# Gated layers of a local-attention block: the 42 features beyond five full tiles, packed two token halves side by side on TensorE

## The chip, the cores and the metric

The kernel runs on one core of one Trainium2 chip, as one launch. The metric is device microseconds of that launch. Five engines are named as in the profile: PE (TensorE matmuls; PEld are its weight loads), DVE (VectorE), ACT (ScalarE), POOL (GpSimd) and SP (SyncE, which issues most DMAs). All data are 32-bit floats.

## The reference, cut to what matters

The network has four stages on 8 sequences of 512 tokens with 256 features: differential attention, a local-attention transformer of two layers, a diffusion stage and a mixture of experts. Only the second half of each layer of the second stage is touched:

```python
HID = int(DIM * 4 * 2 / 3)          # 682
def _layer(x, wqkv, qs, ksc, wo, lg, lb, w1, b1, w2, b2):
    ...
    x = x + o @ wo
    h = shift_token(x)
    mu = h.mean(-1, keepdims=True)
    var = h.var(-1, keepdims=True)
    h = (h - mu) / jnp.sqrt(var + 1e-05) * lg + lb
    h = h @ w1 + b1                 # 256 -> 2 * 682
    a, g = jnp.split(h, 2, axis=-1)
    h = a * jax.nn.gelu(g, approximate=False)
    x = x + h @ w2 + b2             # 682 -> 256
    return x
for l in range(DEPTH):              # DEPTH = 2
    x = _layer(x, ...)
```

682 is five times 128 and 42 left over.

## The kernel before, in words

A tile has 128 partitions (`P`). A sequence is held as four token tiles (`NT = 4`, `S = 512` tokens). The second stage is `local`; it works through 16 combinations of layer and sequence, `combos`, layer 0 for all eight sequences and then layer 1. Three strands are laid into each other by hand: `rotated(c + 1)` (projections, normalised and rotated queries and keys of the next combination), `scores`/`turned`/`attend` (attention of the present one, eight steps `u` as listed in `slots`) and `gated(c - 1)` (output projection and the gated layers of the one before). `rotated` and `gated` are generators; each `yield` ends a part, and `slots` says at which step a part is taken. Within the hand-made order a scheduler sets the final order of each engine's queue.

All matmul results of this stage come from one PSUM pool, `big`, of four buffers, each of two banks (`two` gives a tile of 128 x 2 x 512). The buffers go round, so a new tile waits until the engine that reads the tile four before is done.

`gated` does this for one combination. It multiplies the attention output by `wo` (L680, tile `lpp<-lwo,loT`), adds it to x (L681), moves half the features down by one token with two DMAs into `hs` (L685, L686), normalises (L691), and transposes into `ghT` with ACT applying scale and bias (L694, L546). Then come the gated layers:

- First layer, L697 to L707. For each of six chunks of hidden features, `HCH`, four matmul calls fill a tile `lpa`: two halves (i = 1 the gate, i = 0 the value) by two slices of 128 input features. The stationary operand is a slice of `w1`, the moving one 512 tokens of `ghT`. ACT takes gelu of the gate half (L702, tile `gl`), DVE adds the bias to the value half and multiplies (L703) into `hid` (named `u` in the profile). The sixth chunk has 42 features, so its stationary operand has 42 columns.
- Second layer, L708 to L714. For each pair of token tiles, a tile `lpp` gets for each of the two token tiles six matmul calls of 256 output features, with `hid` as the stationary and `w2` as the moving operand; the sixth chunk has 43 rows, 42 features and a row of ones that carries the bias b2. DVE adds the tile to x (L714).

All these calls go through the helper `mm`, so the profile books them on L200; they are told apart by tile and shape. One matmul call on 32-bit floats appears in the profile as two matmul records with a weight load each: `lpa` has 16 x 6 x 4 = 384 calls and 768 records. Below, "record" means one of these.

The weights of a layer are loaded by `load_local` (L490), by DMAs on SP's queue, into a pool with one buffer for each name; so layer 1 is loaded when `gated(8)` begins, as the last readers of layer 0 let go. The tile `hid` is one buffer for the whole stage; its ones are set once by a memset (L726).

Elsewhere in this stage small operands already share the array: `lsc` (L619) multiplies two heads whose 64 features lie in partitions 0 to 63 and 64 to 127, and `lpo` (L667) writes two heads of 64 features to partitions 0 to 63 and 64 to 127 of one bank.

Of the kernel before, what the change touches and what calls it, by code (L numbers as in the profile page):

```python
# [9 lines left out]
F32 = mybir.dt.float32  # L10
BF16 = mybir.dt.bfloat16
AF = mybir.ActivationFunctionType
ALU = mybir.AluOpType
# [3 lines left out]
P = 128  # L17
NB = 8
NT = 4
S = P * NT  # L20
D = 256
DC = D // P
# [4 lines left out]
FH = 8  # L27
FL = 2
HID = int(D * 4 * 2 / 3)
HCH = [(m, min(P, HID - m)) for m in range(0, HID, P)]  # L30
TH = 16
CH = 8
NE = 8
# [5 lines left out]
HOLD = 1000  # L39
# [77 lines left out]
class Net:  # L117
# [372 lines left out]
    def load_local(self, w, l):  # L490
        nc, a = self.nc, self.a
        g = {}
        g["wo"] = w.tile([P, 4, D], F32, name=f"lwo{l}", tag="wo")
        nc.sync.dma_start(g["wo"], a["L0_ffn_wo"][l].rearrange("(c p) f -> p c f", p=P))
        g["w1"] = w.tile([P, DC, 2 * HID], F32, name=f"lw1{l}", tag="w1")
        nc.sync.dma_start(g["w1"], a["L0_ffn_w1"][l].rearrange("(c p) f -> p c f", p=P))
        n, full = len(HCH), HID // P
        g["w2"] = w.tile([P, n, D], F32, name=f"lw2{l}", tag="w2")
        nc.sync.dma_start(g["w2"][:, :full, :], a["L0_ffn_w2"][l][:full * P].rearrange("(c p) f -> p c f", p=P))
        nc.sync.dma_start(g["w2"][:HID - full * P, full, :], a["L0_ffn_w2"][l][full * P:])  # L500

        nc.sync.dma_start(g["w2"][HID - full * P:HID - full * P + 1, full, :], a["L0_ffn_b2"][l].unsqueeze(0))
        g["b1"] = w.tile([P, 2, n], F32, name=f"lb1{l}", tag="b1")
        for i in range(2):
            b1 = a["L0_ffn_b1"][l][i * HID:(i + 1) * HID]
            with nc.allow_non_contiguous_dma(reason="a bias"):
                nc.sync.dma_start(g["b1"][:, i, :full], b1[:full * P].rearrange("(c p) -> p c", p=P))
                nc.sync.dma_start(g["b1"][:HID - full * P, i, full:], b1[full * P:].unsqueeze(1))
        with nc.allow_non_contiguous_dma(reason="a scale"):
            g["g"] = self.column(w, a["L0_ffn_ln_g"][l], DC, "lg")  # L510
            g["b"] = self.column(w, a["L0_ffn_ln_b"][l], DC, "lb")
        return g

    def local(self, nb, early, first):
# [3 lines left out]
        with ExitStack() as ctx:  # L518
            pool = lambda n, b, **k: ctx.enter_context(self.tc.tile_pool(name=n, bufs=b, **k))
            w = pool("wlocal", 1)  # L520
            wk, small = pool("l_wk", 2), pool("l_small", 4)
            big, dram = pool("l_big", 4, space=PSUM), pool("l_x", 1, space=bass.MemoryType.DRAM)
            nc, tc = self.nc, self.tc
# [4 lines left out]
            two = lambda name: big.tile([P, 2, S], F32, name=name, tag="big")  # L528
# [7 lines left out]
            def flipped(src, dsts, scale=None, bias=None):  # L536

                pt = two("lpt")
                for c in range(DC):
                    for t in range(NT):  # L540
                        nc.tensor.transpose(pt[:, c, self.tok(t)], src[:, t, self.tok(c)], self.ident)
                for c, dst in enumerate(dsts):
                    if scale is None:
                        self.copy(dst, pt[:, c, :])
                    else:
                        nc.scalar.activation(dst, pt[:, c, :], AF.Identity, bias=bias[:, c:c + 1], scale=scale[:, c:c + 1])  # L546
# [110 lines left out]
            def attend(c, h):  # L657
# [10 lines left out]
                                             rhs=pT[:, i, self.tok(t + k)], start=k == max(t - 1, 0), stop=k == t)  # L668
                nc.scalar.copy(attended[c][:, h, :], po[:, 0, :])

            def gated(c):

                l, b = combos[c]
                if l not in rest:
                    rest[l] = self.load_local(w, l)
                g, y = rest[l], self.xb(b)
                oT = attended.pop(c)
                pp = two("lpp").rearrange("p i (t d) -> p (i t) d", d=D)
                for t in range(NT):
                    self.mm(pp[:, t, :], [(oT[:, i, self.tok(t)], g["wo"][:, i, :]) for i in range(4)])  # L680
                nc.vector.tensor_add(y, y, pp)  # L681

                hs = wk.tile([P, NT, D], F32, name="hs", tag="hs", bufs=1)
                nc.gpsimd.memset(hs[0:1, 0, P:D], 0.0)
                nc.sync.dma_start(hs[1:P, :, P:D], y[0:P - 1, :, P:D])  # L685
                nc.sync.dma_start(hs[0:1, 1:NT, P:D], y[P - 1:P, 0:NT - 1, P:D])  # L686
                nc.gpsimd.tensor_copy(hs[:, :, 0:P], y[:, :, 0:P])
                yield

                with tc.issue_after(last[0]), tc.issue_after(last[1]):  # L690
                    self.norm_rows(small, hs, hs)  # L691
                yield
                hT = wk.tile([P, DC, S + 1], F32, name="ghT", tag="hT")
                flipped(hs, (hT[:, 0, 0:S], hT[:, 1, 0:S]), g["g"], g["b"])  # L694
                yield
                rows = [n + (m == len(HCH) - 1) for m, (_, n) in enumerate(HCH)]
                for m, (m0, n) in enumerate(HCH):  # L697
                    pa = two("lpa")
                    for i in (1, 0):
                        self.mm(pa[:n, i, :], [(g["w1"][:, c, i * HID + m0:i * HID + m0 + n], hT[:, c, 0:S]) for c in range(DC)])  # L700
                    gl = wk.tile([P, S], F32, name="gl", tag="gl")
                    gelu = nc.scalar.activation(gl[:n, :], pa[:n, 1, :], AF.Gelu, bias=g["b1"][:n, 1, m:m + 1])  # L702
                    nc.vector.scalar_tensor_tensor(hid[:n, m, :], pa[:n, 0, :], g["b1"][:n, 0, m:m + 1], gl[:n, :], ALU.add, ALU.mult)  # L703
                    if m % 3 == 2:
                        with tc.issue_after(gelu.ins):
                            nc.scalar.preload_act_table_set("natural_log_exp_and_others")
                        yield  # L707
                for t0 in range(0, NT, 2):  # L708
                    if t0:
                        yield  # L710
                    pp = two("lpp").rearrange("p i (t d) -> p (i t) d", d=D)
                    for t in range(2):
                        self.mm(pp[:, t, :], [(hid[:n, m, self.tok(t0 + t)], g["w2"][:n, m, :]) for m, n in enumerate(rows)])
                    nc.vector.tensor_add(y[:, t0:t0 + 2, :], y[:, t0:t0 + 2, :], pp[:, 0:2, :])  # L714
                if l == FL - 1:
                    xs = wk.tile([P, NT, D], F32, name="lx", tag="hs", bufs=1)
                    nc.sync.dma_start(xs, saved[b])
                    self.norm_rows(small, y, y)
                    nc.gpsimd.tensor_add(y, y, xs)

            first, second = Between(), Between()
            r, g = first, second
            total = len(combos)
            self.logs = True
            hid = w.tile([P, len(HCH), S], F32, name="u", tag="u")
            nc.gpsimd.memset(hid[32:64, len(HCH) - 1, :], 1.0)  # L726
            for b in range(min(2, nb)):
                save(b)
            for b in range(min(2, nb)):
# [5 lines left out]
            for c in range(total + 1):  # L735
                if c + 1 < total:
                    r.add(rotated(c + 1))
                for u, calls in enumerate(slots):
                    if c < total:
                        scores(c, u)  # L740
                    if u == 2 and c:
                        g.add(gated(c - 1))
                    half = (len(calls) + 1) // 2
                    for f in calls[:half]:
                        f()
                    before = (c, u - 1) if u else (c - 1, 7)
# [735 lines left out]
```

## Time and profile before

| | |
|---|---|
| time, median of 3 runs | 3997.38 us (3994.92 to 3998.51) |
| the profiled execution, its own time | 3997.02 us |
| its span, first to last instruction | 3995.3 us |
| PE busy | 3578.1 us (90%) |
| DVE, ACT, POOL busy | 2220.8, 1837.3, 1593.6 us (56%, 46%, 40%) |
| mean granted TensorE clock | 0.944 |
| first and last matmul of `lpa` | 1338.6 and 2735.9 us |
| last addition of `lpp` to x (L714) | 2748.5 us |
| DVE L703 on 128 x 512, mean of one | 750 ns |
| ACT gelu L702 on 128 x 512, mean of one | 687 ns |

The stage of the change fills the stretch from about 1176 to 2752 us of the span. Engines work at the same time, so their busy times do not add up; a stretch is bounded by the engine that has no gaps in it, or by the chain of waits through it. [...] what a record takes from PE's time is the distance from its start to the next start.

### The profile page before, as it was taken

How to read it: one execution, taken by the hardware profiler on the slowest of the kernel's cores; microseconds unless marked ns; L12 is line 12 of the kernel's file. 1: busy time of each engine (PE TensorE's matmuls, PEld its weight loads, DVE VectorE, ACT ScalarE, POOL GpSimd, SP SyncE). 2: the span in 40 equal slices, each digit the busy share in tenths (PEclk: the TensorE clock that was granted, in tenths of full speed). 3: DMA queues.
4: the chain of work that ended last, by engine and by line, in shares of the span. 5: the costliest groups of instructions: out<-in, count | busy, mean ns of one | idle time of the engine just before them, and what ended most of it. 6: DMA issues, size and time to landing. Idle time of an engine off the chain costs nothing. (4 is left out here: it accounts for less than half of the span.)

```text
span 3995.3 us, 53421 instructions
## 1 busy us (share of the span) xinstructions
PE 3578.1 (90%) x20002; PEld 1915.7 (48%) x20002; DVE 2220.8 (56%) x4380; ACT 1837.3 (46%) x3671; POOL 1593.6 (40%) x1427
## 2 busy tenths in 40 slices
PE   8999999999978999999999999986988888769985
PEld 3343434443335555555555555553444444446654
DVE  6777767776645666665555555543344343345445
ACT  3555555555434444444444444433554555323334
POOL 3666666666644333333333333311012211143333
PEclk8999999999978999999999999997998999879997
DMA  9200000000000000000000000000000000421114
GB/s 363 87 1 6 6 6 1 6 6 6 6 32 1 3 4 5 4 3 25 9 30 9 9 9 9 9 9 29 6 17 19 25 17 17 133 67 55 54 44 161
DMA packets 92878, 130.46 MB, mean 33 GB/s; under 512 B 23040, under 2 KB 71238, under 8 KB 92614
## 3 DMA queue, kind: packets, MB, share of 16 engines
q1 hardware_dynamic: 86086, 109.10, 8.1%
q0 software_dynamic: 6528, 17.87, 1.3%
q8 instruction: 162, 2.65, 0.3%
q14 instruction: 102, 0.84, 0.1%
HBM read 57.58 MB, written 65.18 MB: 31 GB/s over the span
## 5 line engine op out<-in xcount | busy, mean ns | idle before, releaser
L359 ACT ACTIVATE e<-sa 128x1024 f32<-128x1024 f32 (+3 forms) x512 | 359.2, 702 | 344.6 <-PE sa L352 342.2
L380 POOL TENSOR_TENSOR e<-e,e 128x1536 f32<-128x1536 f32 (+2 forms) x192 | 451.6, 2352 | 93.9 <-PE po L375 83.9
L352 PE MATMUL sa<-qT,kT 32*128 32x512 f32 (+3 forms) x2048 | 435.5, 502 | 8.5 <-ACT e L359 8.1
L342 PE MATMUL sc<-kT,qT 32*128 32x128 f32 (+3 forms) x2048 | 425.4, 498 | 8.8 <-DVE spread L356 5.3
L356 DVE TENSOR_REDUCE spread<-sc 128x2 f32<-128x256 f32 (+3 forms) x512 | 422.2, 825 | 15.3
L200 PE MATMUL lpa<-ghT,lw 128*128 128x512 f32 (+1 forms) x768 | 344.1, 603 | 18.1 <-ACT ghT L546 18.1
L633 ACT ACTIVATE lp<-lp,lnm 128x256 f32<-128x256 f32 (+1 forms) x512 | 240.0, 470 | 261.1 <-DVE lnm L625 165.8
L637 POOL TENSOR_TENSOR lp<-lp,lrs 128x1024 f32<-128x1024 f32 x64 | 121.1, 1893 | 552.3 <-DVE lrs L634 552.3
L355 DVE TENSOR_TENSOR sc<-sc,const 128x256 f32<-128x256 f32 x512 | 218.6, 427 | 163.8 <-PE sa L352 140.3
L342 PEld LDWEIGHTS sc<-kT,qT 32*128 32x128 f32 x2048 | 161.3, 190 | 284.9 <-issue 127.3
L1011 ACT ACTIVATE te<-tsa 128x1024 f32<-128x1024 f32 x256 | 250.3, 1023 | 70.4 <-PE tsa L1007 63.5
L200 PE MATMUL lqk<-qkv,lhT 128*128 128x512 f32 x512 | 245.5, 618 | 2.3 <-DVE qk L584 1.6
L585 POOL TENSOR_TENSOR qk<-qk,over 128x1024 f32<-128x1024 f32 x64 | 151.3, 2365 | 220.8 <-DVE qk L584 220.8
L200 PEld LDWEIGHTS lpa<-ghT,lw 128*128 128x128 f32 (+1 forms) x768 | 134.3, 180 | 212.7 <-issue 169.8
L362 POOL TENSOR_SCALAR_AFFINE_SELECT e<-e 128x512 f32<-128x512 f32 x256 | 160.2, 639 | 174.3 <-ACT e L359 174.2
L1324 ACT ACTIVATE ehT<-eht,enorm 128x128 f32<-128x128 f32 x288 | 108.2, 457 | 209.3 <-PE eht L1320 208.3
L200 PE MATMUL lpp<-lw,u 128*128 128x256 f32 (+1 forms) x768 | 193.2, 396 | 0.0
L375 PE MATMUL po<-e,v 128*32 128x512 f32 (+3 forms) x2048 | 189.1, 453 | 4.0 <-POOL e L362 3.6
L622 DVE TENSOR_TENSOR lp<-lsc,const 128x768 f32<-128x768 f32 (+1 forms) x128 | 138.7, 1083 | 93.2 <-PE lsc L619 93.1
L619 PE MATMUL lsc<-lkT,lqT 64*128 64x256 f32 (+1 forms) x1024 | 158.5, 389 | 27.6 <-DVE qk L584 27.5
L352 PEld LDWEIGHTS sa<-qT,kT 32*128 32x128 f32 x2048 | 160.9, 191 | 43.4 <-ACT e L359 26.7
L1007 PE MATMUL tsa<-tqT,tkT 32*128 32x512 f32 x1024 | 160.4, 675 | 12.6 <-DVE tqT L968 12.0
(278 smaller groups left out, 6850.1 us busy)
## 6 DMA issues: line engine op xcount, KB each, us to landing
xrows<-zero SPq DMA_DIRECT2D x66, 514.0 KB
ex<-xrows SPq DMA_DIRECT2D x72, 128.5 KB
ew<-in_L_ffn_w_dram SPq DMA_DIRECT2D x16, 512.0 KB
egot<-yrows SPq DMA_DIRECT2D x16, 512.0 KB
x<-in_L_attn_X_dram SPq DMA_DIRECT2D x8, 512.0 KB
saved<-x SPq DMA_DIRECT2D x8, 512.0 KB
lx<-saved SPq DMA_DIRECT2D x8, 512.0 KB
xf<-xf SPq DMA_DIRECT2D x8, 512.0 KB
```

Of the source, the lines that this page charges most:

```text
L200: self.nc.tensor.matmul(out, lhsT=l, rhs=r, start=i == 0, stop=i == len(pairs) - 1)
L342: nc.tensor.matmul(sc[:, i, :w], lhsT=qT[g, self.tok(t)], rhs=kT[g, :w], start=True, stop=True)
L352: nc.tensor.matmul(sa[:, i, :S - k * P], lhsT=kT[g, self.tok(k)], rhs=qT[g, k * P:], start=True, stop=True)
L355: nc.vector.tensor_add(sc[:, :, w - P:w], sc[:, :, w - P:w], own)
L356: nc.vector.tensor_reduce(self.spread[n % 2][:, t, g0:g0 + 2, 0 if n % 2 else 16], sc[:, :, :w], AX.X, ALU.max, negate=True)
L359: nc.scalar.activation(x[:, h0:h0 + 2, :], sa[:, :, :S - k * P], AF.Exp, scale=0.25)
L362: nc.gpsimd.affine_select(x[:, :, :P], x[:, :, :P], [[0, 4], [1, P]], ALU.is_ge, 0.0, base=0, channel_multiplier=-1)
L375: nc.tensor.matmul(pos[n][group(g), k * P:], lhsT=seqs[b][1][:, k, 4 * r + g, :], rhs=x[:, g, :], start=k == 0, stop=k == 2)
L380: nc.gpsimd.tensor_add(y, y, es.pop((n, k)))
L633: nc.scalar.activation(x, x, AF.Exp, bias=nm[:, i, k:k + 1], accum_out=rs[:, i, k:k + 1])
L1007: m = nc.tensor.matmul(sa[i // 2][:, i % 2, :], lhsT=kT[q, self.tok(k)], rhs=qT[q, :], start=True, stop=True)
L1011: nc.scalar.activation(e[:, 2 * i:2 * i + 2, :], sa[i], AF.Exp)
```

## The change

The last chunk of 42 features is taken out of the loop over equal chunks. In the first layer its 512 tokens are split into two sets, the tokens of the even and those of the odd token tiles, 256 each. Both sets are multiplied by the same 42 weight columns, filled up with zeros to 64: one call writes its result to partitions 0 to 63 of `lpa`, the other to partitions 64 to 127, in columns 0 to 255. So eight calls of 64 weight columns and 256 tokens stand for four calls of 42 columns and 512 tokens. ACT's gelu works on 128 x 256 for 42 x 512; DVE writes two results of 42 x 256, to partitions 0 to 41 and 64 to 105 of a new tile `left` (named `uleft`), whose rows 42 and 106 are ones.

In the second layer the two token tiles of a pair now have a bank each. Each gets five calls of 128 rows, first the one tile, then the other, and then the two calls of 43 rows follow each other, the first on partitions 0 to 42, the second on 64 to 106. `together` keeps the second call of such a pair right behind the first.

The leftover weights get tiles of their own: `r1` (`lr1`), zeroed by POOL before its DMAs, and `r2` (`lr2`), which holds the 42 rows of w2 and the bias row twice. The bias tile `b1` is zeroed too and holds its last 42 entries twice. `load_local` issues 18 DMAs instead of 11, and POOL gets two memsets per layer; the ones are set by two memsets of 32 x 256 instead of one of 32 x 512.

In the order of PE's queue nothing else changes place: where four leftover calls of `lpa` stood there are eight, and where twelve calls of `lpp` stood there are ten and then two.

```diff
-HCH = [(m, min(P, HID - m)) for m in range(0, HID, P)]
+HF = HID // P
+HR = HID - HF * P
...
+        g["r1"] = w.tile([P, DC, 2, 64], F32, name=f"lr1{l}", tag="r1")
+        g["r2"] = w.tile([P, D], F32, name=f"lr2{l}", tag="r2")
+        nc.gpsimd.memset(g["r1"], 0.0)
+        nc.gpsimd.memset(g["b1"], 0.0)
+        for i in range(2):
+            nc.sync.dma_start(g["w1"][:, :, i], w1[:, :, i, :HF * P])
+            nc.sync.dma_start(g["r1"][:, :, i, :HR], w1[:, :, i, HF * P:])
+        nc.sync.dma_start(g["w2"], a["L0_ffn_w2"][l][:HF * P].rearrange("(c p) f -> p c f", p=P))
+        for j in (0, 64):
+            nc.sync.dma_start(g["r2"][j:j + HR, :], a["L0_ffn_w2"][l][HF * P:])
+
+            nc.sync.dma_start(g["r2"][j + HR:j + HR + 1, :], a["L0_ffn_b2"][l].unsqueeze(0))
...
+            def together(f):
+
+                f(0)
+                with tc.high_priority(offset=HOLD):
+                    tc.keep_in_program_order(f(1))
...
-                rows = [n + (m == len(HCH) - 1) for m, (_, n) in enumerate(HCH)]
-                for m, (m0, n) in enumerate(HCH):
+                for m in range(HF + 1):
                     pa = two("lpa")
                     for i in (1, 0):
-                        self.mm(pa[:n, i, :], [(g["w1"][:, c, i * HID + m0:i * HID + m0 + n], hT[:, c, 0:S]) for c in range(DC)])
+                        if m < HF:
+                            self.mm(pa[:, i, :], [(g["w1"][:, c, i, self.tok(m)], hT[:, c, 0:S]) for c in range(DC)])
+                        else:
+
+                            for c in range(DC):
+                                x = hT[:, c, 0:S].rearrange("p (u j q) -> p j u q", j=2, q=P)
+                                together(lambda j: nc.tensor.matmul(
+                                    pa[64 * j:64 * j + 64, i, 0:2 * P].rearrange("p (u q) -> p u q", q=P),
+                                    lhsT=g["r1"][:, c, i, :], rhs=x[:, j], start=c == 0, stop=c == DC - 1))
+                    n = S if m < HF else 2 * P
                     gl = wk.tile([P, S], F32, name="gl", tag="gl")
-                    gelu = nc.scalar.activation(gl[:n, :], pa[:n, 1, :], AF.Gelu, bias=g["b1"][:n, 1, m:m + 1])
-                    nc.vector.scalar_tensor_tensor(hid[:n, m, :], pa[:n, 0, :], g["b1"][:n, 0, m:m + 1], gl[:n, :], ALU.add, ALU.mult)
+                    gelu = nc.scalar.activation(gl[:, :n], pa[:, 1, :n], AF.Gelu, bias=g["b1"][:, 1, m:m + 1])
+                    for r, dst in ((slice(P), hid[:, m, :]),) if m < HF else ((slice(j, j + HR), left[j:j + HR, :]) for j in (0, 64)):
+                        nc.vector.scalar_tensor_tensor(dst, pa[r, 0, :n], g["b1"][r, 0, m:m + 1], gl[r, :n], ALU.add, ALU.mult)
...
-                    pp = two("lpp").rearrange("p i (t d) -> p (i t) d", d=D)
+                    pp = two("lpp")
                     for t in range(2):
-                        self.mm(pp[:, t, :], [(hid[:n, m, self.tok(t0 + t)], g["w2"][:n, m, :]) for m, n in enumerate(rows)])
-                    nc.vector.tensor_add(y[:, t0:t0 + 2, :], y[:, t0:t0 + 2, :], pp[:, 0:2, :])
+                        for m in range(HF):
+                            nc.tensor.matmul(pp[:, t, 0:D], lhsT=hid[:, m, self.tok(t0 + t)], rhs=g["w2"][:, m, :], start=m == 0, stop=False)
+
+                    together(lambda j: nc.tensor.matmul(pp[:, j, 0:D], lhsT=left[64 * j:64 * j + HR + 1, self.tok(t0 // 2)],
+                                                        rhs=g["r2"][64 * j:64 * j + HR + 1, :], start=False, stop=True))
+                    nc.vector.tensor_add(y[:, t0:t0 + 2, :], y[:, t0:t0 + 2, :], pp[:, :, 0:D])
...
-            hid = w.tile([P, len(HCH), S], F32, name="u", tag="u")
-            nc.gpsimd.memset(hid[32:64, len(HCH) - 1, :], 1.0)
+            hid = w.tile([P, HF, S], F32, name="u", tag="u")
+            left = w.tile([P, 2 * P], F32, name="uleft", tag="uleft")
+            for j in (32, 96):
+                nc.gpsimd.memset(left[j:j + 32, :], 1.0)
```

More of the change, by code (lines that the diff above doesn't have):

```diff
@@ L494, in load_local @@
         nc.sync.dma_start(g["wo"], a["L0_ffn_wo"][l].rearrange("(c p) f -> p c f", p=P))
[L495 to L503, printed above, removed]
+        w1 = a["L0_ffn_w1"][l].rearrange("(c p) (i f) -> p c i f", p=P, i=2)
+        g["w1"] = w.tile([P, DC, 2, HF * P], F32, name=f"lw1{l}", tag="w1")
+        g["w2"] = w.tile([P, HF, D], F32, name=f"lw2{l}", tag="w2")
+        g["b1"] = w.tile([P, 2, HF + 1], F32, name=f"lb1{l}", tag="b1")
+        g["r1"] = w.tile([P, DC, 2, 64], F32, name=f"lr1{l}", tag="r1")
[9 more added lines that the diff above has]
+            nc.sync.dma_start(g["r2"][j + HR:j + HR + 1, :], a["L0_ffn_b2"][l].unsqueeze(0))
         for i in range(2):
@@ L506, in load_local @@
             with nc.allow_non_contiguous_dma(reason="a bias"):
-                nc.sync.dma_start(g["b1"][:, i, :full], b1[:full * P].rearrange("(c p) -> p c", p=P))
-                nc.sync.dma_start(g["b1"][:HID - full * P, i, full:], b1[full * P:].unsqueeze(1))
+                nc.sync.dma_start(g["b1"][:, i, :HF], b1[:HF * P].rearrange("(c p) -> p c", p=P))
+                for j in (0, 64):
+                    nc.sync.dma_start(g["b1"][j:j + HR, i, HF:], b1[HF * P:].unsqueeze(1))
         with nc.allow_non_contiguous_dma(reason="a scale"):
```

## The prediction, made before the changed kernel was run

> **What bounds the kernel now.** I read the table of stages first (columns: stretch, its length, then busy us and records of PE, PEld, DVE, ACT and POOL, then granted clock and DMA), then PE's waits in the same stretch (us in total, times, longest), then PE's order of work within one combination (start, length, idle before).
>
> ```profile
> 1310.00:1400.00 90.00, 87.17 (x447) 53.06 (x445) 55.00 (x88) 41.07 (x104) 31.83 (x23) 0.98 0.01 3
> 1400.00:2000.00 600.00, 572.18 (x2888) 344.68 (x2885) 359.86 (x560) 273.97 (x692) 211.75 (x154) 1.00 0.03 8
> 2000.00:2640.00 640.00, 610.01 (x3098) 372.77 (x3097) 362.19 (x590) 282.28 (x712) 217.18 (x156) 0.98 0.04 12
> ```
>
> ```profile
> PE lsc L619 <- DVE qk L584: 25.4, 14, 1.8
> PE lpt L541 <- DVE hs L181: 18.9, 1, 18.9
> PE lpa L200 <- ACT ghT L546: 18.1, 15, 1.8
> PE lpt L593 <- POOL qk L586: 10.0, 14, 0.7
> ```
>
> PE works 95% of the local stage (572.18 of 600), DVE 60%. Of PE's waits three come once in each combination, 4 us of some 94; one, 18.9 us, comes once at the end. All stand behind the transposes and rotations, none behind `lpa` or `lpp`. So PE's own time in the gated layers is on the path, and what it loses there the span loses.
>
> **What the leftover costs today.** PE's order in one combination, and its weight loads in the first `lpp`:
>
> ```profile
> 1823.74 10.69 PE L200 MATMUL lpa<-ghT,lw 128*128 128x512 f32 x24
> 1834.37 0.88 PE L654 MATMUL lpt<-const,lp 128*128 128x128 f32 x6
> 1835.08 1.04 PE L593 MATMUL lpt<-const,qk 128*128 128x128 f32 x8
> 1836.04 0.93 PE L619 MATMUL lsc<-lkT,lqT 64*128 64x128 f32 x8
> 1836.90 6.03 PE L200 MATMUL lpp<-lw,u 128*128 128x256 f32 x24
> ...
> 1844.76 1.75 PE L667 MATMUL lpo<-lpT,lv 128*64 128x128 f32 x28
> 1846.44 1.14 PE L619 MATMUL lsc<-lkT,lqT 64*128 64x256 f32 x8
> 1847.50 6.03 PE L200 MATMUL lpp<-lw,u 128*128 128x256 f32 x24
> ```
>
> ```profile
> 1836.90 2.02 PEld L200 LDWEIGHTS lpp<-lw,u 128*128 128x128 f32 x10 [0.33 <-DVE lqT L149]
> 1839.25 0.29 PEld L200 LDWEIGHTS lpp<-lw,u 43*128 43x128 f32 x2 [0.33 <-issue]
> 1839.88 2.02 PEld L200 LDWEIGHTS lpp<-lw,u 128*128 128x128 f32 x10 [0.33 <-issue]
> 1842.24 0.29 PEld L200 LDWEIGHTS lpp<-lw,u 43*128 43x128 f32 x2 [0.33 <-issue]
> ```
>
> The reader is to see starts, not lengths. In the second view each block of equal shape stands alone. Ten records of 128 rows take 1836.90 to 1839.25, 2.35 us; two of 43 rows take 1839.25 to 1839.88, 0.63 us. With s for a record of 256 columns and w for one change of shape, 10s + w = 2.35 and 2s + w = 0.63: s = 0.215, w = 0.20 us. So 43 rows cost as much as 128, and each change from full to part of the array and back costs 0.20. One `lpp` is 24s + 4w = 5.96; the first view has 1836.90 to 1842.87, 5.97.
>
> In `lpa` the loads of the 42-column part go from 1830.81, and the next kind of work starts at 1834.37: 3.56 us for eight records of 512 columns, 2 x 0.215 each, plus 0.12 for the change.
>
> **What sharing costs, by rows of this trace.** `lsc` is the pattern of the new second layer: 64-row halves, two banks, two calls after each other. Its eight records of 256 columns take 1846.44 to 1847.50, 1.06 us: four times s plus w, not eight. `lpo` is the pattern of the new first layer: all rows, two sets of 64 columns, one bank. Its 28 records of 128 columns take 1844.76 to 1846.44, 1.68 us: 14 slots of half s (1.51) plus 0.17.
>
> **The sum for one combination.**
> - First layer: sixteen records of 256 columns, two at a time: 8s + 0.15 = 1.87. Saved: 3.56 - 1.87 = 1.69.
> - Second layer, one `lpp`: twenty full records in one block, then four small ones two at a time: 20s + w + 2s + w = 5.13. Saved: 5.97 - 5.13 = 0.84, of which 0.43 is the sharing and 0.40 two changes of shape fewer, since the small calls no longer stand between the two tiles. Twice: 1.68.
> - Together 3.37, and 16 combinations: **53.9 us**.
>
> The stage's clock is 0.98 to 1.00 and 0.86 at its end, which adds under 1 us to a sum made at full clock; I take nothing for it.
>
> **What else moves.**
> - ACT: gelu on 128 x 256 instead of 42 x 512. DVE: two results of 256 columns for one of 512; the row of 512 is 743 ns on 42 partitions as on 128 (750), so width counts, and two of half width cost between 0.74 and twice that. 0.84 is near, since 256-column DVE additions take 418 ns (L1329). It is 0.1 us of an engine idle 40% of the time. Its cover: after the leftover `lpa`, 20 full records (4.3 us) precede the first call that reads `uleft`, against gelu and two products of some 1.4 us. In the last combination `lpp` follows `lpa` at once, and these 4.3 us still cover. Without cover, 0.1 x 16 = 1.6.
> - PSUM: the buffer of the leftover `lpa` comes free later or sooner by 0.2 us; `lpp` takes the buffer after three other tiles. Nothing.
> - POOL: two memsets per layer. In layer 1 the one of `b1` waits for the last L703 of the combination before (about 2023.7); behind it on POOL is L641 at 2028.57, after 10.02 us of idle. Covered by 5 us; if not, `lp` comes late for a transpose that is 10 us off. In layer 0 the memsets stand at 1176.27, where the ones take 0.52 us; I take 0.5 more for the new ones (from 0.1 to 1.0 as they are 12 to 256 wide). `lhT`, behind them, is next used at 1182.11.
> - SP: seven more DMAs per layer, and those of `r1` wait for POOL. In layer 0 all eleven are issued 1176.24 to 1186.97, up to 2.3 us each; seven more end near 1195. Behind them are a copy of x that nothing waits for and then `hs` at 1303.68: 108 us. In layer 1, `w2` is followed by four instead of two small DMAs at 2041.30 to 2042.5; `hs` is at 2054.88. Covered by 11 us.
> - PE: in the first combination of each layer, the two calls of a pair each wait for their own DMA of `r2`, and these waits stand between them, so one pair may not share: 2 x 0.2 us.
>
> Forecast: 3997.0 (this execution) - 53.9 + 0.4 = 3943.5, taken as **3943**. The median of the runs shown, 3997.4, is 0.4 above the profiled one, within their own spread of 3.6.
>
> **Two rules against it.** The Trainium skill, "TensorEngine Tiling (Array Packing)", Key Properties, says that changing the tiling mode drains the array. Read alone it charges the change with new drains: per combination three excursions, six changes of 0.1 us (half of w), 0.6 x 16 = +10. The trace says that the 42-column and 43-row calls of before already pay, five excursions in a combination; after there are three. So the sum has -0.40 where the rule, without the rows, has +0.40 per `lpp`. I take the rows.
>
> The second speaks against the column half. "TensorE: Matmul & The Clock Gate", Part 3, What overlaps and what doesn't, says that a weight load runs beside a matmul in flight only if its row group differs. The two halves of `lpa` have the same rows. By the rule all 16 loads stand in the open; at about 0.14 us each (`lpo`'s loads: 99.3 us for 1792 is 0.055 at least, their mean length 141 ns) they would add 2.2 and the first layer would lose 0.6 instead of gaining 1.69. But `lpo` has that layout, and 28 records with 28 loads took 1.68 us; loads in the open would be 28 x 0.14 = 3.9 alone. The row decides.
>
> **The rivals.**
> - Columns gain nothing, by that rule: rows save 26.9, columns lose 9: 3997 - 18 = **3979**. Against it: `lpo`. For it: `lpo` streams 128 columns per load, this 256, from two pieces of 128 each, a form no row shows.
> - No sharing at all: the two calls run one after the other. Then only the shape changes go: 0.40 x 32 = 13 less, **3984**. Against: the queue keeps the pairs together, as in `lsc`.
> - Half is given back: PE comes earlier to its waits on DVE and POOL and waits longer. Against: those chains start from `lqk` and `lsc`, behind the shortened parts, so they shift along. If half went: **3970**.
> - Slower, by the clock. The first `lpa` block of layer 1 took 12.10 us from start to start where all others took 10.41; in 2089.90 to 2093.30 the granted clock was 0.50. Such a stretch of 3.4 us costs 1.7. Between 1310 and 2600 there are four, each just behind one of the listed waits of PE (for `ghT`, or of `lsc`). If PE, with less to do, met new waits after `lpa` and `lpp`, the clock could fall in every combination. It decides from 54 / 1.7 = 32 more of them, two for each combination. With three in each: 48 x 1.7 = 82, less 54: **4025**. Against: the change puts no wait of PE there, and PE still works 95%.
>
> **How the numbers follow.** Sharing on the path, 3943: 0.80, own range 3936 to 3951. Half given back 0.06, columns gain nothing 0.05, no sharing 0.03: all faster. Slower by the clock 0.04. That everything cancels to within 0.2% (8 us, about what a measurement of this kernel can tell from no change): 0.02. Faster 0.94, same 0.02, slower 0.04. The range for 8 in 10: the ends of the first case are the fits of s and w (10% of 54) and a few half-clock stretches more or less; upward it reaches part of the given-back case: 3935 to 3960.
>
> **What would show it.** Right: the small `lpa` records start in pairs and the block takes about 1.9 us to the next kind of work; one `lpp` takes about 5.1 us; PE's waits keep their list, of 25, 18 and 10 us; PE's busy time falls by some 50 us; stages before 1176 and after 2750 keep their lengths. Wrong: the small block still near 3.5 us (no sharing), a new wait of PE after `lpa` or `lpp` (given back), or a clock under 0.95 in the stage.

## The result, and the profile after

| | before | changed |
|---|---|---|
| time, median (runs) | 3996.15 us | 3945.86 us (3943.64 to 3949.36, 4 runs) |
| ratio to before, 95% interval | | 0.9876 (0.9859 to 0.9893) |
| span of the profiled execution | 3995.3 us | 3941.9 us |
| mean granted TensorE clock | 0.944 | 0.945 |
| PE busy | 3578.1 us | 3521.5 us |

The change gains 50.3 us. The 3996.15 us are runs of the kernel before taken beside the changed one. Twice more the pair was run: 3946.49 against 3994.81 us, ratio 0.9884 (0.987 to 0.9898), and 3945.77 against 3997.16 us, ratio 0.9874 (0.9854 to 0.9895).

The line numbers of the changed kernel are some ten higher: L201 is the helper `mm`, L721 the paired calls of the first layer, L739 and L741 the second layer's full and paired calls, L664 and L551 are the transposes of `lp` and `x`.

First the table of stages of the changed kernel, with columns as before (stretch, its length, busy us and records of PE, PEld, DVE, ACT, POOL, granted clock, DMA):

```profile
1310.00:1400.00 90.00, 87.17 (x458) 53.77 (x457) 56.76 (x90) 41.48 (x107) 31.78 (x23) 0.98 0.01 3
1400.00:2000.00 600.00, 575.60 (x3051) 357.53 (x3050) 369.10 (x578) 283.65 (x711) 214.06 (x159) 0.99 0.03 10
2000.00:2590.00 590.00, 559.81 (x3023) 354.84 (x3023) 352.54 (x581) 267.05 (x683) 213.74 (x152) 0.98 0.03 11
```

PE still works 575.60 of 600 us (the count of records is higher since more combinations fit into 600 us, and since sixteen small records stand for eight in each). The stage stays bounded by PE, so what PE gains at one place does not turn into idle time at another. The list of PE's waits says the same (engine, line, what it waits for: us in total, times, longest):

```profile
PE lsc L629 <- DVE qk L594: 25.3, 14, 1.8
PE lpt L551 <- DVE hs L182: 19.4, 1, 19.4
PE lpa L201 <- ACT ghT L556: 14.5, 15, 1.5
PE lpt L603 <- POOL qk L596: 10.0, 14, 0.7
```

Three of the four are where they were, within 0.5 us (25.4, 18.9 and 10.0 us). The wait for `ghT` is 14.5 instead of 18.1 us; the change did not do that, for a second profile of the kernel before shows 14.6 us in this row.

Now one combination in PE's order of work (start, length, line, tile):

```profile
1803.91 7.13 PE L201 MATMUL lpa<-ghT,lw 128*128 128x512 f32 x16
1810.97 1.95 PE L721 MATMUL lpa<-ghT,lr 128*64 128x256 f32 x16
1812.85 0.87 PE L664 MATMUL lpt<-const,lp 128*128 128x128 f32 x6
1813.56 1.04 PE L603 MATMUL lpt<-const,qk 128*128 128x128 f32 x8
1814.53 0.93 PE L629 MATMUL lsc<-lkT,lqT 64*128 64x128 f32 x8
1815.38 4.58 PE L739 MATMUL lpp<-lw,u 128*128 128x256 f32 x20
1819.90 0.70 PE L741 MATMUL lpp<-lr,uleft 43*128 43x256 f32 x4
1820.53 1.09 PE L664 MATMUL lpt<-const,lp 128*128 128x128 f32 x8
1821.46 1.04 PE L551 MATMUL lpt<-const,x 128*128 128x128 f32 x8
```

Read the starts, not the lengths: a record of 256 columns is listed with some 0.38 us, but the next can start 0.21 us after it. The small block of `lpa` goes from 1810.97 to 1812.85, 1.88 us. Before, it began with this load and the next kind of work started at 1834.37, 3.56 us later:

```profile
1830.81 0.15 PEld L200 LDWEIGHTS lpa<-ghT,lw 128*42 128x42 f32 x2 [0.76 <-ACT gl L702]
```

In the changed kernel the sixteen records start in pairs: 6 to 7 ns apart in a pair, 0.21 us from pair to pair (0.27 after the first). The `lpp` goes from 1815.38 to 1820.53, 5.15 us where 5.97 stood. The weight loads of the same stretch:

```profile
1810.97 1.49 PEld L721 LDWEIGHTS lpa<-ghT,lr 128*64 128x64 f32 x16 [0.76 <-ACT gl L726]
1812.85 0.64 PEld L664 LDWEIGHTS lpt<-const,lp 128*128 128x128 f32 x6 [0.39 <-issue]
1819.89 0.30 PEld L741 LDWEIGHTS lpp<-lr,uleft 43*128 43x128 f32 x4 [0.33 <-issue]
```

All sixteen loads of `lr` lie within the 1.88 us, although both halves of a pair use the same rows. Their 1.49 us cannot stand in the open there, because the eight pairs alone fill 8 x 0.21 = 1.68 us.

From one combination's first `lpa` record to the next one's is 93.87 us before and 90.55 us after, where no drop of the clock falls in between. Two such neighbours of the kernel before, and two of the changed one:

```profile
1807.98 10.57 PE L200 MATMUL lpa<-ghT,lw 128*128 128x512 f32 x24 [1.50 <-ACT ghT L546]
1901.85 10.57 PE L200 MATMUL lpa<-ghT,lw 128*128 128x512 f32 x24 [1.49 <-ACT ghT L546]
```

```profile
1878.70 10.57 PE L201 MATMUL lpa<-ghT,lw 128*128 128x512 f32 x24 [1.50 <-ACT ghT L556]
1969.25 10.57 PE L201 MATMUL lpa<-ghT,lw 128*128 128x512 f32 x24 [1.49 <-ACT ghT L556]
```

That is 3.32 us in each combination, 53.1 in sixteen. By stages, in one profile each:

| stage | before | changed |
|---|---|---|
| differential attention, to the first transpose of `local` | 1179.1 | 1174.8 |
| `local`, to the last record of `lpp` | 1568.9 | 1514.9 |
| diffusion | 786.1 | 785.8 |
| experts | 364.0 | 370.6 |
| rest of the span | 97.1 | 95.8 |

The local stage alone gives the gain, 54.0 us. The experts took 364.0 us in this one profile of before and 370.9 in the other; over all profiles they lie between 364 and 371 us and the first stage between 1173 and 1183, in no order that follows the kernel. That scatter is as large as the distance of a single median from the sum of the stage.

### The profile page after: what moved, and what is told of

It is laid out like the page before. It is cut to its first block, busy times and chain, and to the rows that moved or that the text cites. A ratio compares the mean times of both kernels' runs of the same rounds, so it can differ in the third digit from the quotient of the medians.

```text
span 3941.9 us, 53736 instructions
## 1 busy us (share of the span) xinstructions
PE 3521.5 (89%) x20130; PEld 1906.9 (48%) x20130; DVE 2222.6 (56%) x4396; ACT 1835.3 (47%) x3671; POOL 1595.6 (40%) x1432
## 5 line engine op out<-in xcount | busy, mean ns | idle before, releaser
L201 PE MATMUL lpa<-ghT,lw 128*128 128x512 f32 x640 | 284.8, 600 | 14.5 <-ACT ghT L556 14.5
L201 PE MATMUL lqk<-qkv,lhT 128*128 128x512 f32 x512 | 248.0, 623 | 2.3 <-DVE qk L594 1.6
L201 PEld LDWEIGHTS lpa<-ghT,lw 128*128 128x128 f32 x640 | 119.3, 190 | 165.6 <-issue 136.8
L201 PE MATMUL py<-ew,ehT 128*128 x576 | 146.5, 399 | 23.6 <-ACT ehT L1355 23.6
```

The costliest lines, as they stand in the source:

```text
L201: self.nc.tensor.matmul(out, lhsT=l, rhs=r, start=i == 0, stop=i == len(pairs) - 1)
```

## The experiments

Three questions: does each half of the gain come from where the sum put it; is it the sharing of the array, or only the smaller number of changes of shape; and is there more of the same to be had? All the times, with the interval of the ratio to the kernel before run beside each; the period is that from one combination's first `lpa` record to the next.

| kernel | median us | ratio | period us |
|---|---|---|---|
| before | 3994.81 | 1 | 93.87 |
| changed (again) | 3946.49 | 0.987 to 0.9898 | 90.6 |
| grouped | 3984.65 | 0.9967 to 0.9988 | 93.09 |
| cols_same | 3975.37 | 0.993 to 0.9961 | 92.28 |
| cols_apart | 3960.81 | 0.9901 to 0.9927 | 91.51 |
| cols_by_two | 3948.03 | 0.9868 to 0.9905 | 90.61 |
| rows_apart | 3969.93 | 0.992 to 0.9952 | 92.19 |
| pair_first | 3942.5 | 0.9847 to 0.9885 | 89.87 |
| both_first | 3935.41 | 0.9832 to 0.9872 | 89.72 |

The period is the sharper measure here: it comes from the trace at undisturbed combinations and repeats within 0.05 us, while medians of one kernel differ by a few us.

**again and before_again**: both kernels unaltered, for a second profile of each.

> The changed kernel once more, unaltered, to narrow the interval and to see the stages outside the local one a second time. The profiled pair differed by 54.6 us in the local stage (1179.1 to 2748.0 us before, 1174.8 to 2689.1 after, from the first transpose of x to the last record of lpp), by -4.4 us before it and by +5.5 us after it, while the medians differed by 50.3. Theory A (these outer differences are where the clock's half-speed stretches happened to fall, and are no effect of the change): the medians differ by 50 to 56 us, and the stage after the local one has another length in this profile than 1252.8 us, nearer the 1247.3 of before. Theory B (the change makes the last stages longer): again some 5 us longer than before, and the medians differ by 48 to 50.

> The kernel of before, unaltered, for a second profile of its stages. If its last stage and its first are as scattered as in the profiles so far (experts 364 to 371 us, first stage 1175 to 1183), the local stage is the only one that the change moves: 1566 to 1572 us here against 1515 in both profiles of the changed kernel.

Measured 3946.49 us with a span of 3944.5, and 3995.21 us (one run) with a span of 3993.5. Local stages 1515.0 and 1566.3 us: the gain of this stage is 51 to 54 us by these four profiles. Everything after the local stage took 1246.7 us in the second profile of the changed kernel, near the 1247.3 of before, as Theory A said. The medians, 48.3 us apart, fell short of its 50 to 56 and lie in Theory B's 48 to 50, though B's longer last stages did not come.

**grouped**: the kernel before, its second layer put in the new order but with nothing to share. Five full calls for one token tile, five for the other, then the two of 43 rows, both on the same rows.

```diff
-                    for t in range(2):
-                        self.mm(pp[:, t, :], [(hid[:n, m, self.tok(t0 + t)], g["w2"][:n, m, :]) for m, n in enumerate(rows)])
+                    for part in (list(enumerate(rows))[:-1], list(enumerate(rows))[-1:]):
+                        for t in range(2):
+                            for m, n in part:
+                                nc.tensor.matmul(pp[:, t, 0:D], lhsT=hid[:n, m, self.tok(t0 + t)], rhs=g["w2"][:n, m, :],
+                                                 start=m == 0, stop=m == len(rows) - 1)
```

> The kernel of before with the order of the second layer alone altered: five full calls for the one token tile, five for the other, then the two 43-row calls, both on the same rows of the array, so nothing can be shared. Theory A (each change between the full array and a part of it costs 0.20 us): one lpp 24 x 0.215 + 2 x 0.20 = 5.56 us instead of 5.96, 32 times, 12.8 us less than before in all. Rival (the 0.20 belongs to each small call, by its few rows, and not to the change): nothing is saved, within 3 us of before.

Measured 10.2 us below the kernel before (by the interval 4.8 to 13.2), and 0.78 us in each period, 12.5 in sixteen. One `lpp`, from its start to that of the next kind of work, takes 5.57 us, where 5.97 stood and 5.56 were expected:

```profile
1834.54 5.64 PE L715 MATMUL lpp<-lw,u 128*128 128x256 f32 x24
1840.11 1.09 PE L654 MATMUL lpt<-const,lp 128*128 128x128 f32 x8
```

So a quarter of the gain has nothing to do with side by side: it comes from not letting the small calls stand between two blocks of full ones.

**rows_apart**: the changed kernel, each small call of the second layer put behind its own token tile's five full ones.

```diff
                         for m in range(HF):
...
-                    together(lambda j: nc.tensor.matmul(pp[:, j, 0:D], lhsT=left[64 * j:64 * j + HR + 1, self.tok(t0 // 2)],
-                                                        rhs=g["r2"][64 * j:64 * j + HR + 1, :], start=False, stop=True))
+                        nc.tensor.matmul(pp[:, t, 0:D], lhsT=left[64 * t:64 * t + HR + 1, self.tok(t0 // 2)],
+                                         rhs=g["r2"][64 * t:64 * t + HR + 1, :], start=False, stop=True)
```

> The changed kernel, but in the second layer each small call stands behind the five full calls of its own token tile, as before the change. Theory A: sharing and two changes of shape are lost in each lpp, which goes from 5.15 back to 5.96 us; 0.81 x 32 = 26 us slower than the changed kernel. Rival (the second layer was hidden behind waits and gave less than its share): under 20 us slower.

Measured 23.4 us above the changed kernel. Its order of work shows the old picture, a small block after each full one:

```profile
1823.34 2.43 PE L739 MATMUL lpp<-lw,u 128*128 128x256 f32 x10
1825.70 0.70 PE L740 MATMUL lpp<-lr,uleft 43*128 43x256 f32 x2
1826.33 2.42 PE L739 MATMUL lpp<-lw,u 128*128 128x256 f32 x10
1828.68 0.70 PE L740 MATMUL lpp<-lr,uleft 43*128 43x256 f32 x2
```

1823.34 to 1825.70 and 1825.70 to 1826.33 are the 2.36 and 0.63 us of the kernel before, to 0.01. The period is 1.64 us longer than the changed kernel's (92.19 - 90.55), 26.2 in sixteen. This is the whole worth of the second layer; less the 0.78 of **grouped**, 0.86 us are the sharing itself, two `lpp` of 0.43.

**cols_apart**: the eight calls of the first layer's leftover put in another order, all of the left half, then all of the right.

```diff
-                            for c in range(DC):
-                                x = hT[:, c, 0:S].rearrange("p (u j q) -> p j u q", j=2, q=P)
-                                together(lambda j: nc.tensor.matmul(
...
+                        calls = [(j, i, c) for j in range(2) for i in (1, 0) for c in range(DC)]
+                        for k, (j, i, c) in enumerate(calls):
```

> The changed kernel, but in the first layer all four calls on the one half of the array's columns, then all four on the other. Same calls, same loads, same data. Theory A (the gain of the first layer comes from two calls running side by side): the sixteen records take 15 to 16 slots of 0.215 plus 0.15, some 3.4 to 3.6 us instead of 1.88, so 24 to 27 us slower than the changed kernel. Rival (the gain comes from half the tokens per call, or from the packing of the result): no slower than the changed kernel by more than 3 us.

A miss: it should have lost the whole sharing and lost 14.3 us against the changed kernel, some 0.96 us in each period. The block:

```profile
1811.96 7.13 PE L201 MATMUL lpa<-ghT,lw 128*128 128x512 f32 x16
1819.03 2.86 PE L722 MATMUL lpa<-ghT,lr 128*64 128x256 f32 x16
1821.82 0.87 PE L664 MATMUL lpt<-const,lp 128*128 128x128 f32 x6
```

1819.03 to 1821.82 is 2.79 us, neither 1.88 nor 3.6. A single record does not name its half, but the sixteen starts form two series of eight, 0.21 to 0.27 us from start to start, and in the program built from this kernel PE's queue holds the four left calls, then the four right ones. So the first of the right half is the one at 1819.950. It starts together with the fifth of the left half at 1819.944, though three of the left half that came before it in the queue had not started. PE did not keep to the order of its queue between the two halves, and the experiment did not take away what it was to take away. Two more kernels followed from that.

**cols_same**: both sets of tokens write to partitions 0 to 63, so that no order lets them run side by side. Calls, columns and loads are as many as in the changed kernel; gelu works on 64 x 512, and the two products read one partition range. PE's list of waits has no new row, so neither reaches the path.

```diff
-                                together(lambda j: nc.tensor.matmul(
-                                    pa[64 * j:64 * j + 64, i, 0:2 * P].rearrange("p (u q) -> p u q", q=P),
-                                    lhsT=g["r1"][:, c, i, :], rhs=x[:, j], start=c == 0, stop=c == DC - 1))
+                            for j in range(2):
...
+                                    nc.tensor.matmul(pa[0:64, i, 2 * P * j:2 * P * j + 2 * P].rearrange("p (u q) -> p u q", q=P),
+                                                     lhsT=g["r1"][:, c, i, :], rhs=x[:, j], start=c == 0, stop=c == DC - 1)
```

> The changed kernel, but in the first layer both token halves of the leftover go to the same half of the array's columns (partitions 0 to 63 of the PSUM tile, side by side in its columns); gelu then works on 64 x 512, and DVE's second product writes from partitions 0 to 41 to partitions 64 to 105. Same number of calls, loads and columns, no second place for them to run. In the experiment before this one, where the halves only stood apart in the queue, PE let the second half start when the first was half done, and the block took 2.80 us. Theory A (the gain is two calls side by side, and nothing else of the edit): sixteen slots of 0.215 plus 0.15 to 0.2, 3.6 us, 1.7 more than the changed kernel per combination; period of a combination 90.55 + 1.7 = 92.3, and 27 us slower in all. Rival (half of the gain is smaller calls or the empty columns): under 20 us slower.

Measured 3975.37 us, 29 above the changed kernel's 3946. That one is from another comparison; the ratios to before, 0.9945 and 0.9884, make it 24 us. The block of the same sixteen records:

```profile
1824.79 3.67 PE L722 MATMUL lpa<-ghT,lr 128*64 128x256 f32 x16
1828.38 0.88 PE L664 MATMUL lpt<-const,lp 128*128 128x128 f32 x6
```

The next kind of work starts 3.60 us later (3.598 before rounding). Same calls, same weights, same 256 tokens for each load: only the columns of the array differ, and 1.88 becomes 3.60. The period is 1.73 us longer than the changed kernel's, 27.7 in sixteen.

**cols_by_two**: the order of halves changed less, two calls left, two right, then again. Theory A is that PE looks some records ahead and starts one whose part of the array is free; the rival is that records start in the order of the queue, so that only neighbours at the seams can overlap.

```diff
+                        calls = [(j, i, c) for i in (1, 0) for j in range(2) for c in range(DC)]
```

> The changed kernel with the eight small calls of the first layer ordered two and two: two calls (four records) on the left columns, two on the right, two left, two right. In the kernel with the halves wholly apart the first record of the right columns started together with the fifth of the left, so three records of the left that stood ahead of it in the queue were passed. Theory A (PE looks some three or four records ahead and starts what finds its part of the array free): all sixteen records pair up but for the first and last few, the block takes 1.9 to 2.2 us, and the time is that of the changed kernel within 5 us. Rival (records start in the order of the queue, and the earlier overlap came from the end of a call): only neighbours at the seams can overlap, 13 slots of 0.215 plus 0.15, 2.9 us, 16 us slower than the changed kernel.

```profile
1811.21 2.00 PE L722 MATMUL lpa<-ghT,lr 128*64 128x256 f32 x16
1813.14 0.87 PE L664 MATMUL lpt<-const,lp 128*128 128x128 f32 x6
```

1.93 us against 1.88 (the rival: 2.9), and 2.3 us in the time, which the intervals do not tell from nothing. In the built program the queue holds two left calls, then two right ones. The right half's first record starts 13 ns after the left's first, past three left ones ahead of it. Theory A held. In **cols_apart** the right half's first has eight left ones ahead and starts when three are still to come. Both fit a view of about three records ahead; how deep it is was not tried further.

**pair_first**: the changed kernel with the small pair of each `lpp` ahead of the full calls instead of behind them. It then follows `lsc`, which uses half the rows too.

```diff
                     pp = two("lpp")
+                    together(lambda j: nc.tensor.matmul(pp[:, j, 0:D], lhsT=left[64 * j:64 * j + HR + 1, self.tok(t0 // 2)],
+                                                        rhs=g["r2"][64 * j:64 * j + HR + 1, :], start=True, stop=False))
                     for t in range(2):
                         for m in range(HF):
-                            nc.tensor.matmul(pp[:, t, 0:D], lhsT=hid[:, m, self.tok(t0 + t)], rhs=g["w2"][:, m, :], start=m == 0, stop=False)
-
-                    together(lambda j: nc.tensor.matmul(pp[:, j, 0:D], lhsT=left[64 * j:64 * j + HR + 1, self.tok(t0 // 2)],
-                                                        rhs=g["r2"][64 * j:64 * j + HR + 1, :], start=False, stop=True))
+                            nc.tensor.matmul(pp[:, t, 0:D], lhsT=hid[:, m, self.tok(t0 + t)], rhs=g["w2"][:, m, :], start=False, stop=m == HF - 1)
```

> The changed kernel with one thing moved: in each lpp the two 43-row calls come first, right behind the 64-row calls of lsc, and the ten full calls after them. Theory A (a change of shape costs 0.20, wherever it stands; from lsc to the pair there is none): 0.20 x 32 = 6.4 us faster than the changed kernel, period 90.15. Rival (the pair now waits for uleft, which DVE finishes some 1.3 us after lpa, or the array drains all the same because the calls are other ones): no gain, or up to 1 us lost per combination.

```profile
1812.72 0.93 PE L629 MATMUL lsc<-lkT,lqT 64*128 64x128 f32 x8
1813.48 0.60 PE L737 MATMUL lpp<-lr,uleft 43*128 43x256 f32 x4
1814.01 4.58 PE L741 MATMUL lpp<-lw,u 128*128 128x256 f32 x20
1818.43 1.04 PE L664 MATMUL lpt<-const,lp 128*128 128x128 f32 x8
1819.31 1.04 PE L551 MATMUL lpt<-const,x 128*128 128x128 f32 x8
```

The period is 0.68 us shorter than the changed kernel's, more than the 0.40 expected. Compare with the changed kernel's rows above: `lsc` takes 0.76 instead of 0.85, `lpp` 4.95 instead of 5.15, and the transposes behind it 0.88 instead of 0.93. The expectation forgot that the transpose after the pair also pays for a change of shape. Around one `lpp` three changes become one, together 0.34 us, twice in a combination. The time, 3942.5 us, lies 3 to 4 us below the changed kernel's, which the intervals do not tell from nothing; here the period decides. The rival's wait for `uleft` did come, but only after 2590 us, 1.4 us in all.

**both_first**: also the leftover of `lpa` as the fourth of six chunks, so that it follows `lsc` and not a full chunk.

```diff
-                for m in range(HF + 1):
+                for k, m in enumerate((0, 1, 2, HF, 3, 4)):
...
-                    if m % 3 == 2:
+                    if k % 3 == 2:
```

> As the pair-first kernel, and the leftover chunk of the first layer is moved from sixth to fourth place, between lsc and the two full chunks, so that one change of shape less is met there too. Theory A: a further 0.15 to 0.20 per combination, 2.4 to 3.2 us, 9 us faster than the changed kernel in all, period 89.97. Rival (gelu and products of the later full chunks now end the chain into lpp, and PE waits for DVE): no faster than the pair-first kernel.

```profile
1800.69 1.95 PE L721 MATMUL lpa<-ghT,lr 128*64 128x256 f32 x16
1802.57 7.13 PE L201 MATMUL lpa<-ghT,lw 128*128 128x512 f32 x16
1809.54 0.82 PE L664 MATMUL lpt<-const,lp 128*128 128x128 f32 x6
1810.19 1.04 PE L603 MATMUL lpt<-const,qk 128*128 128x128 f32 x8
```

The small block still takes 1.88 us (1800.69 to 1802.57): it uses another part of the array than `lsc` (128 rows by 64 columns, not 64 by 128). What goes is one change of shape, since a full block now leads straight into the transposes: the full block takes 6.97 instead of 7.06 us and the transposes behind it 0.65 instead of 0.71. That is the 0.15 us that goes from the period, against **pair_first**. In the time the two are not told apart, as their intervals overlap. To be sure of the better version, it was run again beside the changed kernel on the same chip, both unaltered.

> The changed kernel, unaltered, as the yardstick for the two kernels beside it: 3944 to 3949 us, 48 to 54 less than before.

> The both-first kernel once more, beside the changed one on one chip. In the profiles its period is 89.74 us against 90.55, of which 0.68 is the pair moved behind lsc (three changes of shape less one around each lpp, two of 0.15 to 0.20, not the one that was expected) and 0.15 the leftover chunk. Theory: 16 x 0.83 = 13 us faster than the changed kernel, 9 to 16 with the scatter of such runs. Rival (the earlier result was a favourable set of runs): within 5 us of it.

Measured 3945.77 and 3934.48 us: 11.3 us faster than the changed kernel, against 0.83 x 16 = 13.3 by the period. Its ratio to before is 0.9846 (0.9829 to 0.9864). The single runs hardly overlap (3926.51 to 3938.52 against 3938.30 to 3948.83 us). This version beats both kernels.

## Why the prediction was right, point by point

| term of the sum, us in one combination | predicted | measured | by |
|---|---|---|---|
| first layer, columns side by side | 1.69 | 1.73 (1.68) | cols_same against changed (blocks of before and changed) |
| second layer, two changes of shape fewer, twice | 0.80 | 0.78 | before against grouped |
| second layer, rows side by side, twice | 0.86 | 0.86 | rows_apart against changed, less the line above |
| all | 3.37 | 3.32 | before against changed |

The measured terms add up to 3.37 and not to 3.32, since the block of **cols_same** takes 3.60 us where the kernel before had 3.56. The 0.05 us that the prediction missed are one `lpa` block of 1.88 for 1.87 and two `lpp` of 5.15 for 5.13.

- **PE is the bound.** Held. 54.0 us went from the local stage in the first pair of profiles for the 53.9 predicted, and the list of waits stayed. That the two agree to 0.1 us is luck: over all pairs of profiles the stage gives 51 to 57.
- **`lpo` and `lsc` are the patterns of what is new.** Held: blocks of 1.88 and 5.15 us for 1.87 and 5.13. The rival "columns gain nothing" (3979) rested on the page "TensorE: Matmul & The Clock Gate", Part 3, What overlaps and what doesn't; the loads in the 1.88 us above speak against it. So do rows of before that the prediction shows: ten loads of all 128 rows, 2.02 us, lie within the 2.35 us of ten records that at 0.215 fill 2.15 of them. And **cols_same**, where a gain is really absent, shows what it would have looked like.
- **The changes of shape.** Held, and **grouped** gives their price alone: 0.78 / 4 = 0.195 us for each of the four taken away (0.20). The rule of "TensorEngine Tiling (Array Packing)", Key Properties, that a change of mode drains the array is not contradicted. What the trace of before added is that calls of 43 rows pay it even when nothing stands beside them, so the change took changes away. The +10 us that the prediction set against itself is a slip: it takes six changes at half of w, while its own fit and **grouped** give w, 0.20 us, for each. The rule read alone would have charged 6 x 0.20 x 16 = 19 us.
- **"No sharing at all"** (3984) is what **grouped** ran at, 3984.65 us, with both layers unshared. The changed kernel is 38 us below it.
- **Half given back** (3970). Did not happen: the period fell by 3.32 of the 3.37 us.
- **The clock.** It did not happen. Before the long stretch at half clock near the end of the stage (17.07 us, from 2625.82 before and from 2573.64 in the changed kernel), the changed kernel has six stretches at half clock from 1310 us on and the kernel before four, each of 3.41 us. But the second profile of the kernel before has six too, and the other two of the changed kernel five and six: their number follows the profile, not the change. One of before, in windows of the profile (granted clock third from the end), and the block that it fell on:

```profile
2089.90:2093.30 3.40, 3.40 (x4) 1.44 (x5) 1.97 (x4) 2.64 (x10) 3.32 (x2) 0.50 0.04 16
```

```profile
2089.86 12.26 PE L200 MATMUL lpa<-ghT,lw 128*128 128x512 f32 x24 [1.77 <-ACT ghT L546]
```

  Here the stretch begins just after PE's wait and costs the full 1.70: that period is 95.57 us. Most others cost 0.40 (94.27 for 93.87 before, 90.95 for 90.55 after). Where such a stretch lies ahead of the wait for `ghT`, the wait shrinks from 1.5 to 0.3 us and takes up the rest. So one stretch was priced four times too high in most places, and the rival would have needed not 32 but some 135 of them (54 / 0.40). What sets their number was not tried. The profiles show a pattern: within each, the starts of these stretches lie whole multiples of 3.413 us apart (before: 224, 52 and 55 of them), and in the 3.41 us ahead of each PE waits for 1.70 us or more, most often the 1.8 us of `lsc`. That is not enough by itself, for some intervals with as much waiting are not followed by one. It would explain why the number changes from profile to profile: how the waits fall on that grid changes too.
- **Small costs.** The estimate of 0.5 us for POOL's memsets in layer 0 measured 0.55 (1.07 in all for 0.52). In layer 1, the memsets wait as foreseen and `lp` still waits for DVE long after them (start, length, idle before and its releaser):

```profile
1994.10 0.31 POOL L503 MEMSET lr<- 128x256 f32 x1 [2.01 <-PE lpa L721]
1995.68 0.11 POOL L504 MEMSET lb<- 128x12 f32 x1 [1.27 <-DVE uleft L728]
2000.42 1.61 POOL L651 TENSOR_TENSOR lp<-lp,lrs 128x256 f32<-128x256 f32 x2 [4.64 <-DVE lrs L644]
```

  4.64 us of idle are left behind them, so they cost nothing there. DVE's two products took 0.98 us in that combination's row, for 0.84 predicted; nothing waits for them. SP's loads of layer 1 were over 12 us ahead of the next transfer on the queue. The unpaired first pair, 2 x 0.2 us, did not come: in all 32 `lpp` of the changed kernel's profile the first two small records start 6 to 7 ns apart.
- **What is left open.** The medians moved by 50.3, 48.3 and 51.4 us, the sum said 53.5. The local stage gives 51 to 57 over the profiles taken. As single runs of the kernel before go from 3981 to 4007 us, whether 2 to 5 us are really lost somewhere, or are scatter of the first stage and the experts, can't be told.

## What to carry to other kernels

Where an engine has no gaps in a stage, price a change from starts in that stage, and find in the trace a row with the same pattern of the array before believing a rule about it; here two such rows gave the gain in the period to 2%. A matmul on a part of the array costs twice: its own time, and a change of shape on each side (0.12 to 0.20 us each here). So first group small matmuls (a quarter of the gain here), then let them share, then place them next to other small ones, as **both_first** does for another 11 us. To test whether two calls share, give them the same part of the array; changing their order is not enough.

## What the runs showed that was not expected

- PE did not start records strictly in the order of its queue when they lay on different columns of the array: in **cols_apart** a record started past three waiting ones, and in **cols_by_two** 13 ns after the first, past three, so that the block lost only 0.05 us.
- Weight loads of column halves with the same rows ran beside the matmuls: 16 loads of 64 columns within 1.88 us that eight pairs at 0.21 already fill.
- A half-clock stretch of 3.41 us cost 0.40 us in most combinations, and 1.70 only right behind the wait that else would take it up. Its start always lay a whole multiple of 3.413 us from the others of the same profile.
